# Weight loads and field 0 in ring order, field loads one by one, and more splits dealt out: a pairwise bilinear kernel on one core

## The chip, the cores and the metric

The kernel runs on one core of a Trainium2 chip. The metric is the device time of one execution in microseconds (us). Three executions before the change took 749.28, 749.29 and 749.32 us; the median is 749.29 us.

A core has a matrix engine (PE, with its weight loads as PEld), a vector engine (DVE), an activation engine (ACT), a general engine (POOL) and a sync engine (SP) that here only issues DMA transfers. Transfers run on 16 DMA engines, whoever issues them.

## What is computed

There are 1024 samples of 32 fields with 128 numbers each, and one 128 x 128 matrix for each of the 496 pairs of fields i < j. For every sample and pair, field i is multiplied by the pair's matrix, and the result is multiplied element by element with field j:

```python
v_i = inputs[:, I_IDX, :]
v_j = inputs[:, J_IDX, :]
transformed = jnp.einsum('bpd,ped->bpe', v_i, W)
return transformed * v_j
```

In float32 the inputs are 16.8 MB, the matrices 32.5 MB and the output 260 MB. Much of what follows is about the stores of that output.

## The kernel before the change

**Order of the work.** The pairs are numbered q = 0 to 495, from field i = 30 down to field 0, and for each i over j = i + 1 to 31. Field i has 31 - i pairs, and they begin at `first_q[i]`, which is (30 - i)(31 - i)/2: field 17 begins at 91, field 12 at 171, field 0 at 465. The main loop (L243) counts half-pairs u = 2q + h; each half is a tile of 128 x 512 (512 samples). `first(u)` issues the first matmuls, `second(u)` the last one and the multiplication by field j, three half-pairs later.

**Splits.** The first 15 pairs are multiplied in plain float32 (L216). All others use three faster matmuls (L219 twice, L228 once) on operands that have been split into parts: a high part, a low part and a difference. `split_w` splits a weight chunk of two pairs: one operation on ACT (L128) and three on POOL (L129 to L131). `split_x` splits one half of field i: one on ACT (L145), two on POOL (L146, L147), and the difference on DVE (L273) for fields 10 to 25 or on POOL (L151) for fields 0 to 9. All splits stand in a list `todo` with the pair from which each may be issued and its deadline; at every odd u the ready one with the earliest deadline is issued. A weight chunk is ready five pairs before its first use. A field's halves are ready one pair into the field before; for fields 1 to 11 (`SPREAD`) they are moved on by 1/5 and 3/5 of that field's length.

**Weights.** Eight pairs make one weight load of 512 KB, numbered c = 0 to 61, in a ring of three buffers (`WB`). A load of chunk c can start once the last split of the chunk that held its buffer has read it. Even chunks from 12 on (`WAPART`) are fetched in two parts (L103, L104): 448 KB issued by POOL[...], 64 KB by SP. They are asked for in the loop as soon as the last split of chunk c - 3 has been issued (L269). Odd chunks are asked for at fixed pairs `w_at`, in general at 8c - 17 (L182 to L186); chunks 55 and 57, the odd ones among the first three after `XAFTER`, come at 8c - 11. [...]

**Fields.** Fields 31 to 17 are loaded one by one at the start and through the first pairs. Fields 16 to 1 are loaded in four groups of 2 MB at pairs 52, 141, 219 and 313 (`XAT`): `load_group` fetches four fields in one transfer from a copy that the host has laid out in rows of 16 KB. Field 0 borrows one of the three weight buffers, at pair 421 (`x_at`).

**Output buffers.** A store takes four pairs, 2 MB, and is issued on ACT's queue (L263). Three output buffers (`s0` to `s2`) are always there. The four group tiles serve as output buffers too until 20 pairs before their fields are loaded (`until`), so the number falls from seven to three, for the last time at pair 293.

**Queues.** SP issues its transfers in program order, and waits at each for its buffer: the fields, the odd chunks and the 64 KB parts stand in one line. POOL issues its parts between its splits. PE, ACT, DVE and POOL also work strictly in program order.

Of the kernel before, what the change touches and what calls it, by code (L numbers as in the profile page):

```python
# [7 lines left out]
F32 = mybir.dt.float32  # L8
# [3 lines left out]
P = 128  # L12
NF = 32
NQ = NF * (NF - 1) // 2
BT = 1024
HB = 512
WC = 2
WL = 8
# [3 lines left out]
SHARED = 16  # L22
XDLAG = 10
LAG = 3
SPREAD = 12
WB = 3
WLEAD = 12
XAFTER = 54
XLEAD = 5

XG = 4
NE = 14
ROWS = 8 * NE
WAPART = tuple(range(12, 62, 2))
BACK = 3
XAT = (313, 219, 141, 52)
OWAIT = 20
SLAG = 2


# [6 lines left out]
def kernel(  # L47
# [22 lines left out]
    nc = tc.nc  # L70
# [3 lines left out]
    xpool = ctx.enter_context(tc.tile_pool(name="x", bufs=1))  # L74
# [6 lines left out]
    x_sb = {}  # L81

    def load_x(f, pieces=1, eng=None):
        if f == 0:

            t = rpool.tile([P, WL, P], F32, tag="w", name="x_0").rearrange("p q e -> p (q e)")
        else:
            t = xpool.tile([P, BT], F32, tag=f"x{f}", name=f"x_{f}")
        s = BT // pieces
        for k in range(pieces):  # L90
            (eng or nc.sync).dma_start(out=t[:, k * s : (k + 1) * s], in_=xt[f, :, k * s : (k + 1) * s])
        x_sb[f] = t

    w_raw = {}
# [3 lines left out]
    def move_on(k):  # L98

        nc.gpsimd.dma_start(out=mark[: 2 * k], in_=xt[0, : 2 * k, :16].rearrange("(b a) n -> a b n", a=k))  # L100

    def load_apart(dst, src):
        nc.gpsimd.dma_start(out=dst[:ROWS], in_=src[:ROWS].rearrange("(b a) m n -> a b m n", a=NE))  # L103
        nc.sync.dma_start(out=dst[ROWS:], in_=src[ROWS:])  # L104

    def load_group(k):
        t = xpool.tile([P, XG, BT], F32, tag=f"g{k}", name=f"x_g{k}")
        f = XG * k + 1
        nc.sync.dma_start(out=t, in_=xt[f : f + XG].rearrange("m d b -> (m d b)").rearrange("(d m b) -> d m b", m=XG, b=BT))
        for m in range(XG):  # L110
            x_sb[f + m] = t[:, m, :]

    def load_w(c, splits=(0, WL), eng=nc.sync):
        w_raw[c] = rpool.tile([P, WL, P], F32, tag="w", name=f"w_{c}")
        if c in WAPART:
            load_apart(w_raw[c], wt[c])
            return
        for a, b in zip(splits, splits[1:]):
            eng.dma_start(out=w_raw[c][:, a:b, :], in_=wt[c, :, a:b, :])

    w_s, spent = {}, []
# [17 lines left out]
    def split_x(f, a, u):  # L139

        if a == 0:
            x_s[f] = [spool.tile([P, BT], F32R, tag=t, name=f"{t}_{f}") for t in ("xh", "xl", "xd")]
        s = slice(a, a + HB)
        h, l, d = [t[:, s] for t in x_s[f]]
        nc.scalar.mul(h, x_sb[f][:, s], 1.0 - 2.0**-13)  # L145
        nc.gpsimd.tensor_tensor(l, x_sb[f][:, s], h.bitcast(F32), ALU.subtract)  # L146
        nc.gpsimd.tensor_scalar(l, l.bitcast(F32), 1.0 / EPS, 1.0, ALU.mult, ALU.mult)  # L147
        if f > NF - 2 - NATIVE - SHARED:
            later.append((min(u + XDLAG, 2 * first_q[f] + LAG - 1), d, h.bitcast(F32), l.bitcast(F32)))
        else:  # L150
            nc.gpsimd.tensor_tensor(d, h.bitcast(F32), l.bitcast(F32), ALU.subtract)  # L151
# [3 lines left out]
    first_q = {i: q for q, (i, j) in reversed(list(enumerate(pairs)))}  # L155
# [6 lines left out]
    for i in range(NF - 2 - NATIVE, -1, -1):  # L162
        for a in range(0, BT, HB):
            at = first_q[i + 1] + 1 if i < NF - 3 - NATIVE else 2
            if 0 < i < SPREAD:
                at += (NF - 2 - i) * (1 + 2 * (a > 0)) // 5
            todo.append((at, first_q[i], lambda u, i=i, a=a: split_x(i, a, u)))
    todo.sort(key=lambda t: t[1])

# [5 lines left out]
    load_w(1, eng=nc.sync)  # L175
    for f in range(NF - 5, NF - 4 - XLEAD, -1):
        load_x(f)
# [3 lines left out]
    w_at = {}  # L181
    for c in range(WB, -(-NQ // WL)):  # L182
        free = (c - WB + 1) * WL if (c - WB) * WL < nq0 else 0
        early = 0 if XAFTER < c <= XAFTER + WB else WLEAD - 6
        if c not in WAPART:
            w_at[max(c * WL - 3 * WC - 5 - early, free)] = c  # L186
    x_at = XAFTER * WL - 11
    assert x_at not in w_at and len(w_at) == NQ // WL - WB - len(WAPART)

    back = []  # L190
    w_next = list(WAPART)

    ngroup = NF // XG // 2
    group_at = {q: k for k, q in enumerate(XAT)}
    assert all(q < first_q[XG * k + XG + 1] for q, k in group_at.items())
    until = {f"g{k}": q - OWAIT for q, k in group_at.items()}
    used = {t: n - 9 for n, t in enumerate(("s0", "s1", "s2", *sorted(until, reverse=True)))}

    def out_tile(g):
# [9 lines left out]
    def first(u):  # L209
        q, h = divmod(u, 2)  # L210
        i, c = pairs[q][0], q // WC
        r = slice(q % WC * P, (q % WC + 1) * P)
        s = slice(h * HB, (h + 1) * HB)
        po[u] = ppool.tile([P, HB], F32, tag="po", name=f"po_{u}")
        if q < nq0:
            nc.tensor.matmul(po[u], w_raw[q // WL][:, q % WL, :], x_sb[i][:, s], start=True, stop=True)  # L216
        else:
            for t in (0, 1):
                nc.tensor.matmul(po[u], w_s[c][t][:, r], x_s[i][t][:, s], start=t == 0, stop=t == 1)  # L219
            nc.scalar.mul(po[u], po[u], 1.0 + EPS)  # L220

    def second(u):
        q, h = divmod(u, 2)
        i, j = pairs[q]
        r = slice(q % WC * P, (q % WC + 1) * P)
        s = slice(h * HB, (h + 1) * HB)
        if q >= nq0:
            nc.tensor.matmul(  # L228
                po[u], w_s[q // WC][2][:, r], x_s[i][2][:, s], start=False, stop=True, skip_group_check=True
            )  # L230
        g, k = divmod(q, OG)
        if k == 0 and h == 0:
            ots[g] = out_tile(g)
        nc.vector.tensor_tensor(ots[g][:, k, s], po.pop(u), x_sb[j][:, s], ALU.mult)  # L234
        if q >= NQ - 2:
            stores.append((u + SLAG, out[g, :, k, s], ots[g][:, k, s]))
        elif g == 0 or q >= NQ - OG:
            if h == 1:
                stores.append((u + SLAG, out[g, :, k], ots[g][:, k]))
        elif k == OG - 1 and h == 1:  # L240
            stores.append((u + SLAG, out[g], ots[g]))

    for u in range(2 * NQ + LAG + SLAG):  # L243
        q = u // 2
        if u < 2 * NQ:
            i, j = pairs[q]
            if u % 2 == 0 and j == i + 1 and XG * ngroup < i - 2 - XLEAD:
                load_x(i - 2 - XLEAD)
            first(u)
            if u == 2 * nq0:  # L250
                move_on(5)
            if u % 2 == 0 and q in group_at:
                load_group(group_at[q])
            if u % 2 == 1 and q in w_at:
                load_w(w_at[q])
            if u % 2 == 0 and q in back:
                move_on(16 - NE if w_next else 13)
            if u == 2 * x_at + 1:
                load_x(0)
        if LAG <= u < 2 * NQ + LAG:  # L260
            second(u - LAG)
        while stores and stores[0][0] <= u - LAG:
            nc.scalar.dma_start(*stores.pop(0)[1:])  # L263
        if u % 2 == 1:
            ready = [t for t in todo if t[0] <= q]
            if ready:
                ready[0][2](u)
                todo.remove(ready[0])
        if w_next and (XAFTER if w_next[0] == XAFTER + 2 else w_next[0] - WB) in spent:  # L269
            load_w(w_next.pop(0))  # L270
            back.append(q + BACK)
        while later and later[0][0] <= u:
            nc.vector.tensor_tensor(*later.pop(0)[1:], ALU.subtract)  # L273
    assert not todo and not later and not stores
# [32 lines left out]
```

## Time and profile before

| What | Value |
|---|---|
| Median of three executions | 749.29 us |
| Profiled execution | 752.84 us |
| Its span, first to last instruction | 751.1 us |
| PE busy | 703.7 us (94%) |
| DVE busy | 662.8 us (88%) |
| ACT busy | 625.7 us (83%) |
| POOL busy | 614.9 us (82%) |
| Moved by DMA | 310.06 MB, mean 413 GB/s |
| Mean granted PE clock | 0.981 |

The page divides the span into 40 slices of 18.8 us. Of each engine it gives the busy share, of PE also the granted clock, and of the DMA engines the busy share and what they moved. A share close to one on several engines at once says little here; what matters is which wait ends last in a given stretch. The costliest groups of instructions, with count and mean length:

| Line | Engine | What | Count | Mean ns |
|---|---|---|---|---|
| L219, L228 | PE | matmuls of the split pairs | 2886 | 393 to 396, overlapping |
| L220 | ACT | scaling between the matmuls | 962 | 583 |
| L234 | DVE | product with field j | 992 | 684 to 685 |
| L129, L130, L131 | POOL | split of a weight chunk | 241 each | 762, 416, 744 |
| L146, L147 | POOL | split of a field's half | 52 each | 1315, 675 |
| L151 | POOL | difference, fields 0 to 9 | 20 | 1288 |
| L273 | DVE | difference, fields 10 to 25 | 32 | 970 |

Of the transfers, a 2 MB store takes 12.4 us from issue to landing (median), a 512 KB weight load of SP's 10.6 us, POOL's part of an even chunk 11.8 us, and a 2 MB group of fields 18.0 us.

### The profile page before, as it was taken

The numbers are of one execution on the slowest core, as the hardware profiler recorded it, in microseconds if no ns is written. First come the engines' busy times: TensorE is split into PE (matmuls) and PEld (weight loads), VectorE is DVE, ScalarE is ACT, GpSimd is POOL, SyncE is SP. The second block draws the span as 40 slices with busy tenths as digits, with TensorE's granted clock in tenths as the row PEclk, the third lists the DMA queues.
The fourth block names the chain that finished last, engine by engine and source line by source line (L and its number), as shares of the span: only waits on it lengthen the run. The fifth ranks groups of instructions, "written<-read, shape, count | busy, mean of one in ns | idle before, by whom it ended". The sixth has DMA issues, their size and how long they took to land.

```text
span 751.1 us, 11065 instructions
## 1 busy us (share of the span) xinstructions
PE 703.7 (94%) x2946; PEld 556.8 (74%) x2946; DVE 662.8 (88%) x1024; ACT 625.7 (83%) x1256; POOL 614.9 (82%) x902
## 2 busy tenths in 40 slices
PE   7998999899999999996999979799999999889994
PEld 3576777777787788885887858688877777668883
DVE  3899999999999999986998869699888888779995
ACT  1198989889999999995999959689988889779993
POOL 1789999999999989986999968869898888797660
PEclk9999999999999999999999989899999999999997
DMA  9999999999999999999999999999999999989998
GB/s 344 430 421 430 407 428 428 426 402 414 403 420 426 426 424 423 427 419 421 427 423 427 423 416 385 426 406 414 419 426 419 408 422 405 403 340 420 419 424 344
DMA packets 32941, 310.06 MB, mean 413 GB/s; under 512 B 5104, under 2 KB 5232, under 8 KB 16752
## 3 DMA queue, kind: packets, MB, share of 16 engines
q10 hardware_dynamic: 19584, 261.10, 82.8%
q1 hardware_dynamic: 8864, 36.77, 12.3%
q0 software_dynamic: 4432, 11.48, 4.3%
q8 instruction: 24, 0.39, 0.2%
q14 instruction: 37, 0.30, 0.1%
HBM read 49.29 MB, written 260.05 MB: 412 GB/s over the span
## 4 chain that ended last, share of the span: by engine, by line
PE 65%; DMA 18%; DVE 7%; POOL 6%; issue 1%; ACT 1%; DVEq 0%; ACTq 0%; POOLq 0%
PE po L219 41%; PE po L228 20%; DMA out_dram<-ot 18%; DVE ot L234 6%; PE po L216 4%; POOL wl L129 2%; POOL xl L146 1%; POOL wd L131 1%; ACT po L220 1%; POOL xl L147 1%; DMA x<-in_xt_dram 1%; POOL xd L151 1%; POOL wd L130 0%; DVE xd L273 0%; ACT wh L128 0%
## 5 line engine op out<-in xcount | busy, mean ns | idle before, releaser
L220 ACT ACTIVATE po<-po 128x512 f32<-128x512 f32 x962 | 544.9, 583 | 90.1 <-PE po L219 51.4
L234 DVE TENSOR_TENSOR ot<-po,x 128x512 f32<-128x512 f32 x720 | 463.1, 684 | 61.6 <-DMA out_dram<-ot 33.8
L219 PE MATMUL po<-xh,wh 128*128 128x512 f32 x962 | 380.5, 396 | 19.9 <-DVE ot L234 19.8
L219 PE MATMUL po<-xl,wl 128*128 128x512 f32 x962 | 379.6, 395 | 10.9 <-POOL wl L129 9.5
L228 PE MATMUL po<-xd,wd 128*128 128x512 f32 x962 | 377.6, 393 | 1.8 <-DVE xd L273 0.9
L219 PEld LDWEIGHTS po<-xh,wh 128*128 128x128 f32 x962 | 182.5, 190 | 66.4 <-DVE ot L234 28.1
L129 POOL TENSOR_TENSOR wl<-w,wh 128x256 fp32r<-128x256 f32 x241 | 183.6, 762 | 55.8 <-ACT wh L128 51.5
L219 PEld LDWEIGHTS po<-xl,wl 128*128 128x128 f32 x962 | 182.5, 190 | 53.6 <-POOL wl L129 14.5
L228 PEld LDWEIGHTS po<-xd,wd 128*128 128x128 f32 x962 | 182.6, 190 | 41.9 <-ACT po L220 2.7
L131 POOL TENSOR_TENSOR wd<-wl,wd 128x256 fp32r<-128x256 f32 x241 | 179.4, 744 | 20.1
L234 DVE TENSOR_TENSOR ot<-po,x_g 128x512 f32<-128x512 f32 x272 | 174.6, 685 | 17.3 <-DMA out_dram<-ot 10.1
L130 POOL TENSOR_SCALAR wd<-wh 128x256 fp32r<-128x256 f32 x241 | 100.2, 416 | 20.5
L128 ACT ACTIVATE wh<-w 128x256 fp32r<-128x256 f32 x241 | 99.1, 412 | 9.9 <-DVE ot L234 5.4
L146 POOL TENSOR_TENSOR xl<-x_g,xh 128x512 fp32r<-128x512 f32 x32 | 42.1, 1315 | 0.5
L146 POOL TENSOR_TENSOR xl<-x,xh 128x512 fp32r<-128x512 f32 x20 | 26.3, 1316 | 15.8 <-ACT xh L145 15.6
L147 POOL TENSOR_SCALAR xl<-xl 128x512 fp32r<-128x512 f32 x52 | 35.1, 675 | 4.7
L216 PE MATMUL po<-x,w 128*128 128x512 f32 x60 | 30.4, 666 | 4.2 <-DMA x<-in_xt_dram 4.0
L273 DVE TENSOR_TENSOR xd<-xh,xl 128x512 fp32r<-128x512 f32 x32 | 31.0, 970 | 0.2 <-POOL xl L147 0.2
L216 PEld LDWEIGHTS po<-x,w 128*128 128x128 f32 x60 | 12.4, 212 | 21.4 <-issue 14.1
L151 POOL TENSOR_TENSOR xd<-xh,xl 128x512 fp32r<-128x512 f32 x20 | 25.8, 1288 | 1.7
L145 ACT ACTIVATE xh<-x 128x512 fp32r<-128x512 f32 x20 | 12.4, 627 | 11.5 <-DMA x<-in_xt_dram 11.4
L145 ACT ACTIVATE xh<-x_g 128x512 fp32r<-128x512 f32 x32 | 20.0, 626 | 0.0
(7 smaller groups left out, 33.8 us busy)
## 6 DMA issues: line engine op xcount, KB each, us to landing
out_dram<-ot ACTq DMA_DIRECT2D x122, 2048.0 KB, 12.4
w<-in_wt_dram SPq DMA_DIRECT2D x36, 512.0 KB, 10.6
w<-in_wt_dram POOLq DMA_DIRECT2D x25, 448.0 KB, 11.8
x_g<-in_xt_dram SPq DMA_DIRECT2D x4, 2048.0 KB, 18.0
x<-in_xt_dram SPq DMA_DIRECT2D x14, 512.0 KB, 9.4
out_dram<-ot ACTq DMA_DIRECT2D x6, 512.0 KB, 8.3
w<-in_wt_dram SPq DMA_DIRECT2D x26, 64.0 KB, 6.1
x<-in_xt_dram ACTq DMA_DIRECT2D x4, 256.0 KB, 6.0
```

The costliest lines, as they stand in the source:

```text
L128: nc.scalar.mul(h, raw, 1.0 - 2.0**-13)
L129: nc.gpsimd.tensor_tensor(l, raw, h.bitcast(F32), ALU.subtract)
L130: nc.gpsimd.tensor_scalar(d, h.bitcast(F32), EPS, 1.0, ALU.mult, ALU.mult)
L131: nc.gpsimd.tensor_tensor(d, l.bitcast(F32), d.bitcast(F32), ALU.subtract)
L146: nc.gpsimd.tensor_tensor(l, x_sb[f][:, s], h.bitcast(F32), ALU.subtract)
L147: nc.gpsimd.tensor_scalar(l, l.bitcast(F32), 1.0 / EPS, 1.0, ALU.mult, ALU.mult)
L151: nc.gpsimd.tensor_tensor(d, h.bitcast(F32), l.bitcast(F32), ALU.subtract)
L216: nc.tensor.matmul(po[u], w_raw[q // WL][:, q % WL, :], x_sb[i][:, s], start=True, stop=True)
L219: nc.tensor.matmul(po[u], w_s[c][t][:, r], x_s[i][t][:, s], start=t == 0, stop=t == 1)
L220: nc.scalar.mul(po[u], po[u], 1.0 + EPS)
L228: nc.tensor.matmul(po[u], w_s[q // WC][2][:, r], x_s[i][2][:, s], start=False, stop=True, skip_group_check=True)
L234: nc.vector.tensor_tensor(ots[g][:, k, s], po.pop(u), x_sb[j][:, s], ALU.mult)
```

## The change

There are three edits.

1. All weight chunks from 12 on, odd ones too, and field 0 are asked for in one list `ring`, in order: each when the last split that reads the buffer it takes over has been issued. Field 0 stands between chunks 54 and 55, and its own second split frees its buffer for chunk 57. Before, 57 came at pair 445, after 58.
2. Fields 16 to 1 are loaded one by one, 512 KB each, six pairs apart (`XSTEP`), highest field first, into the same four group tiles; the host no longer lays groups out in long rows. The pairs of `XAT` are those of the first load of each four.
3. The halves of fields 17 to 12 are dealt out as well (`SPREAD` 18), and the shares of the field's length are 1/5 and 1/2 in place of 1/5 and 3/5, for fields 1 to 11 too.

```diff
-SPREAD = 12
+SPREAD = 18
+WRING = 12
+XSTEP = 6
...
-    def load_group(k):
-        t = xpool.tile([P, XG, BT], F32, tag=f"g{k}", name=f"x_g{k}")
-        f = XG * k + 1
-        nc.sync.dma_start(out=t, in_=xt[f : f + XG].rearrange("m d b -> (m d b)").rearrange("(d m b) -> d m b", m=XG, b=BT))
-        for m in range(XG):
-            x_sb[f + m] = t[:, m, :]
+    group = {}
+
+    def load_group(k, m):
+        if m == XG - 1:
+            group[k] = xpool.tile([P, XG, BT], F32, tag=f"g{k}", name=f"x_g{k}")
+        f = XG * k + 1 + m
+        x_sb[f] = group[k][:, m, :]
+        nc.sync.dma_start(out=x_sb[f], in_=xt[f])
...
+        if f == 0 and a > 0:
+            spent.append("x")
...
-                at += (NF - 2 - i) * (1 + 2 * (a > 0)) // 5
+                at += (NF - 2 - i) * (2 + 3 * (a > 0)) // 10
...
-        early = 0 if XAFTER < c <= XAFTER + WB else WLEAD - 6
-        if c not in WAPART:
-            w_at[max(c * WL - 3 * WC - 5 - early, free)] = c
-    x_at = XAFTER * WL - 11
+        if c < WRING:
+            w_at[max(c * WL - 3 * WC + 1 - WLEAD, free)] = c
...
-    w_next = list(WAPART)
+    last = NQ // WL
+    ring = [*range(WRING - WB, XAFTER + 1), "x", *range(XAFTER + 1, last)]
...
-    group_at = {q: k for k, q in enumerate(XAT)}
+    group_at = {q + XSTEP * (XG - 1 - m): (k, m) for k, q in enumerate(XAT) for m in range(XG)}
...
-            if u == 2 * x_at + 1:
-                load_x(0)
...
-        if w_next and (XAFTER if w_next[0] == XAFTER + 2 else w_next[0] - WB) in spent:
-            load_w(w_next.pop(0))
-            back.append(q + BACK)
+        if ring[WB:] and ring[0] in spent:
+            ring.pop(0)
+            c = ring[WB - 1]
+            if c == "x":
+                load_x(0)
+            else:
+                load_w(c)
+            if c in WAPART:
+                back.append(q + BACK)
...
-    for f in range(1, XG * 4, XG):
-        xt[f : f + XG] = xt[f : f + XG].transpose(1, 0, 2).copy().reshape(XG, P, BT)
```

More of the change, by code (lines that the diff above doesn't have):

```diff
@@ L183 @@
         free = (c - WB + 1) * WL if (c - WB) * WL < nq0 else 0
-        early = 0 if XAFTER < c <= XAFTER + WB else WLEAD - 6
-        if c not in WAPART:
-            w_at[max(c * WL - 3 * WC - 5 - early, free)] = c
-    x_at = XAFTER * WL - 11
-    assert x_at not in w_at and len(w_at) == NQ // WL - WB - len(WAPART)
+        if c < WRING:
+            w_at[max(c * WL - 3 * WC + 1 - WLEAD, free)] = c
     back = []
-    w_next = list(WAPART)
+    last = NQ // WL
+    ring = [*range(WRING - WB, XAFTER + 1), "x", *range(XAFTER + 1, last)]
     ngroup = NF // XG // 2
-    group_at = {q: k for k, q in enumerate(XAT)}
-    assert all(q < first_q[XG * k + XG + 1] for q, k in group_at.items())
-    until = {f"g{k}": q - OWAIT for q, k in group_at.items()}
+    group_at = {q + XSTEP * (XG - 1 - m): (k, m) for k, q in enumerate(XAT) for m in range(XG)}
+    assert all(q + 5 < first_q[XG * k + m + 2] for q, (k, m) in group_at.items())
+    until = {f"g{k}": q - OWAIT for k, q in enumerate(XAT)}
     used = {t: n - 9 for n, t in enumerate(("s0", "s1", "s2", *sorted(until, reverse=True)))}
@@ L252 @@
             if u % 2 == 0 and q in group_at:
-                load_group(group_at[q])
+                load_group(*group_at[q])
             if u % 2 == 1 and q in w_at:
@@ L256 @@
             if u % 2 == 0 and q in back:
-                move_on(16 - NE if w_next else 13)
-            if u == 2 * x_at + 1:
-                load_x(0)
+                move_on(16 - NE if max(w_raw) < WAPART[-1] else 13)
         if LAG <= u < 2 * NQ + LAG:
```

## The prediction

> **What bounds the kernel now.** I read the page's slices first, then the busy times over stretches, the waits in each stretch, and last the timelines of POOL, DVE and SP where a stretch loses time.
>
> ```profile
> DMA  9999999999999999999999999999999999989998
> GB/s 344 430 421 430 407 428 428 426 402 414 403 420 426 426 424 423 427 419 421 427 423 427 423 416 385 426 406 414 419 426 419 408 422 405 403 340 420 419 424 344
> q10 hardware_dynamic: 19584, 261.10, 82.8%
> q1 hardware_dynamic: 8864, 36.77, 12.3%
> ```
>
> The DMA engines are never free, and the best slices reach 430 GB/s. 310.06 MB at 430 GB/s are 721 us, so about 30 us of the 751.1 us span are slices below that rate. Those slices fall in three stretches with three causes.
>
> Stretch A, 44 to 262 us. The waits there, and POOL's timeline:
>
> ```profile
> ACT po L220 <- PE po L219: 11.7, 14, 2.1
> PEld po L219 <- POOL wl L129: 11.5, 10, 2.5
> PE po L219 <- POOL wl L129: 7.3, 9, 2.0
> DVE ot L234 <- PE po L228: 2.7, 4, 1.4
> POOL wl L129 <- ACT wh L128: 0.7, 1, 0.7
> ```
>
> ```profile
> 195.15 0.62 POOL L103 DMA_DIRECT2D w<-in_wt_dram  x1
> 195.80 1.30 POOL L146 TENSOR_TENSOR xl<-x_g,xh 128x512 fp32r<-128x512 f32 x1
> 197.19 0.62 POOL L147 TENSOR_SCALAR xl<-xl 128x512 fp32r<-128x512 f32 x1
> 197.88 0.74 POOL L129 TENSOR_TENSOR wl<-w,wh 128x256 fp32r<-128x256 f32 x1
> ```
>
> PE waits for POOL, POOL waits once (0.7 us), and DVE never waits for a store here. POOL is the bound, back to back; DVE's full digits are its 0.685 us operations keeping PE's pace of 0.68 us a unit (the listed matmul starts of one kind lie 0.68 apart). DMA takes what comes: 406 GB/s from 150.0 to 206.5 us.
>
> Stretch B, 300 to 638 us, is the stores':
>
> ```profile
> 337.00:356.00 19.00, 13.06 (x50) 10.00 (x49) 10.96 (x18) 10.29 (x22) 11.66 (x17) 0.91 1.01 423
> 432.00:450.00 18.00, 12.91 (x48) 9.97 (x47) 10.55 (x18) 10.09 (x22) 12.56 (x19) 0.81 1.00 422
> 450.00:469.00 19.00, 19.00 (x86) 15.73 (x85) 18.87 (x29) 17.91 (x37) 15.45 (x23) 1.00 0.98 382
> 469.00:488.00 19.00, 14.84 (x58) 11.85 (x57) 12.07 (x20) 12.43 (x26) 15.46 (x24) 0.88 1.01 424
> 488.00:545.00 57.00, 57.00 (x248) 47.00 (x248) 52.11 (x81) 52.77 (x107) 47.14 (x70) 0.98 1.01 414
> ```
>
> ```profile
> 444.33 4.40 DVE L234 TENSOR_TENSOR ot<-po,x 128x512 f32<-128x512 f32 x7 [5.95 <-DMA out_dram<-ot]
> 483.35 4.40 DVE L234 TENSOR_TENSOR ot<-po,x 128x512 f32<-128x512 f32 x7 [6.09 <-DMA out_dram<-ot]
> ```
>
> (Columns: busy us and count of PE, PEld, DVE, ACT, POOL, then granted clock, DMA share, GB/s.) PE loses 5 us in each stall, yet DMA moves 422 to 424 GB/s through it: the stall itself is free. What costs is the stretch after it, at 382 and 414 GB/s, where PE restarts slowly and the stores run out. The stalls near 340 and 483 us follow the 2 MB group loads issued at 329.43 and 462.87; the one at 444 comes as output buffers fall from four to three (pair 293).
>
> Stretch C, 638 to 676 us (372 GB/s), is W chunk 55 landing late (ACT waits 2.7 us), with field 0's splits in POOL's way behind it.
>
> **What the Trainium skill says.** "DMA: Bandwidth & Descriptors", Queues, rings and completion order: an SDMA engine takes its queue rows in turn, packet by packet. The trace agrees: where 4 KB weight rows meet stores of 16 KB rows (439 to 444 us) the sum stays at 417 GB/s. The same page, "Issuing engines are not separate DMA queues", says that all issuers share 16 engines, so moving loads about adds no bandwidth; 430 GB/s in slices of very different mix agrees. "TensorE: Matmul & The Clock Gate", Part 1: after an idle window of about 3.4 us the clock halves until PE has been busy as long. Here the granted clock was 0.81 in 432 to 450 us.
>
> **The change part by part.**
>
> (1) Odd weight chunks from 13 on are asked for up to six pairs earlier in program order. But SP runs ahead and waits for the buffer: its waits at L119 for POOL wl are 365.4 us in 32. For instance chunk 55 was issued at 641.25, as the `wl` of 640.48 + 0.74 ended. The buffer's last reader is the same after the change, and the SP order of the chunks too, save at the end. Price 0 on SP; POOL's loads of even chunks keep their place. What was hidden stays hidden.
>
> (2) Field 0 in the ring: chunk 57 takes field 0's buffer (free at 664.24, as `xl` ended) instead of chunk 55's (669.01), and 58 takes the other. Chunk 57's first split is chunk of pairs 228, near 680 us, so neither was late. Price 0. If PE were ahead by 8 us it would matter; it is not.
>
> (3) Spreading fields 17 to 12. POOL's work is the same, so in a stretch that POOL fills the gain is in order alone. Today weight DMA, first half, one weight chunk, mark and second half come together: from 195.15 to the end of the next chunk at 205.0 POOL finishes two weight chunks in 9.9 us, where PE uses one in 2.72 us. It loses 9.9 - 5.4 = 4.5 us of lead and wins 2.72 - 2.02 = 0.7 us back per chunk (chunks start 2.02 us apart in a gapless run). With the new formula the second half comes two to four chunks later than now, so 1.4 to 2.8 us of lead are won back between the halves, the dip is that much shallower, and PE can run that much nearer to POOL. I take 1.5, the size of the one DVE bubble there (1.40 at 144.00). Deadline: field 17's second half began at 139.87 and was first used about 8.7 us later; four pairs of 1.36 us later still leave 3 us, against 2.0 us of `xl` work (1.31 + 0.68). After it the DMA is next in line; from 150 to 206.5 us it has room (406 against 430), so the gain passes. Range 0 to -2.8.
>
> (4) Halves of fields 11 to 1 come 2 or 3 pairs earlier. Field 1's second half (637.14 to 640.5) stands just ahead of the split that frees chunk 55's buffer. One chunk sooner, that release comes some 0.8 us earlier, out of ACT's 2.7 us wait: -0.5, range +0.3 to -1.
>
> (5) Four 2 MB loads of 16 KB rows become sixteen of 512 KB with 4 KB rows, six pairs apart. SP issues 4 x 0.33 = 1.3 us for each old 1.15: nothing. Each lands in about 10 us (the weight loads' 10.6) and is needed 12 pairs (16 us) or more later: no wait. On the DMA: q10 needs 0.828 x 751.1 / 261.10 = 2.38 us per MB, q1 with its mix 2.51; taking the 8.4 MB of groups out at q10's price leaves 2.55 for q1's small rows, so 8.4 MB get dearer by at most 8.4 x 0.17 = 1.4 us, at least 0 where they interleave. I take +0.4. In return the stores keep most of each engine's turns, the 6.09 us stall at 483 us splits into pieces of about 1.2 us (512 KB at 425 GB/s), PE stays at full clock, and the shortfall after it shrinks: 57 us x (1 - 414/425) = 1.5 us, of which I take half, -0.8. The stall at 340 us goes too, but brings nothing, as stores were queued. The one at 444 us is not touched. Range of this part -1.5 to +4.8, the upper end from the rival below.
>
> Sum: 0 + 0 - 1.5 - 0.5 + 0.4 - 0.8 = -2.4 us. The profiled execution took 752.84 us (span 751.1); the plain runs' median is 749.29. I take the difference over unchanged: 746.9.
>
> **Rivals.**
>
> *The stores swallow it.* From 206 us on DMA is at 422 to 428 GB/s, so A's gain may only lengthen the queue, and the buffers fill sooner. For: the waits for stores from 304 us on. Against: the hole at 150 to 206 us. Result: +0.4 - 0.8 remain, at about 748.9.
>
> *Single reads run into an empty store queue (slower).* A weight read that comes when few stores are queued runs all engines at once and slowly: 621 to 624 us had 302 GB/s, 457 to 460 had 320, so 0.8 us is lost against 425. The eight single loads of fields 8 to 1 would each cost that, 6.4 us, less the two bursts' own aftermath (about 2), so +4.4; with A's -1.5, C's -0.5 and the dearer rows' +0.4 that is +2.8, or 752.1. It decides from the fifth of the eight that falls into such a gap (0.8 x 5 - 2 - 1.6 = +0.4). For: three output buffers from pair 293 on. Against: while a queue exists, reads interleave at 417.
>
> *The stalls matter more than I think.* DVE's waits from the groups are 3.37 + 4.66 and 0.56 + 6.09 = 14.7 us. If half came off the end: 742. Against: DMA moved 423 GB/s through them.
>
> **How the numbers follow.** Main case 0.51, around 746.9 (745.3 to 748.5): faster 0.44, same 0.07. Swallowed 0.18: same. Slower rival 0.20: 0.18 slower, 0.02 same. Large gain 0.11: faster. Together faster 0.55, same 0.27, slower 0.18, where 0.2% (1.5 us) is what a measurement of this kernel tells from none. The range 743.4 to 751.6 leaves out the lower half of the large gain and the upper half of the slower rival, with what lies past all cases.
>
> **What would show it.** Part 3: POOL still without gaps to about 260 us, but PE's waits for `wl` in 112 to 262 us well below now, and pairs there done 1 to 2 us earlier. Part 5: no DVE wait of 6 us near 483 us, several near 1 us, clock at 1.0, and over 414 GB/s in 488 to 545 us. Parts 1 and 2: SP's issues of odd chunks still at the ends of `wl`. Wrong if PE's waits for POOL move but do not shrink, or if slices after 450 us fall below today's rates wherever an x read lies.

## The result, and the profile after

The first comparison gave 745.91 us for the changed kernel and 749.20 us for the kernel before (medians of 12 executions each), a ratio of 0.9966 with a 95% interval of 0.9946 to 0.9987. A ratio takes in all executions, so it is not the quotient of the two medians: 0.9966 stands for 2.5 us, while the medians lie 3.3 us apart. The forecast was 746.9 us against 749.29, a ratio of 0.9968. Two further comparisons on the same footing gave less: 0.9987 (0.9968 to 1.0006) and 0.9995 (0.9970 to 1.0020). Weighted by their intervals the three come to about 0.9982, give or take 0.0012, or 1.4 us faster. That is below the 1.5 us at which the forecast drew its line, and the sum of the single parts is no better known. So all three point the way that was forecast, but only the first interval leaves out no change, and the size is little more than half of the first figure. As the experiments show, the gain of the forecast's main term did not reach the end.

The page of the changed kernel, with the lines that answer to those of before:

```profile
DMA  9999999999999999999999999999999999999998
GB/s 344 426 422 430 428 428 425 428 427 420 426 422 426 422 422 429 424 425 423 425 427 424 422 427 348 417 424 425 423 427 390 424 419 421 427 422 417 424 418 330
q10 hardware_dynamic: 19584, 261.10, 83.3%
q1 hardware_dynamic: 10592, 36.77, 12.3%
```

The low slices between 75 and 206 us are gone (402 to 414 before, 420 to 428 now), and so is the one at 657 to 676 us. But slice 25, from 446 to 465 us, has fallen to 348. The span is 743.7 us against 751.1.

This 7.4 us difference of two single traces must not be read as the effect. 2.3 us of it lie before pair 20, where the two kernels do the same. The rest lies after pair 313, at about 470 us: up to there, counted from pair 20, the two are level (429.8 and 429.6 us). Counted in the same way to the end, the three traces of the changed kernel alone take 704.6, 706.2 and 709.7 us, so they differ by as much among themselves.

What waited in the changed kernel from 44 to 262 us (engine and line waited for: us in total, times, longest):

```profile
ACT po L224 <- PE po L223: 9.2, 14, 1.5
PEld po L223 <- POOL wl L133: 7.7, 11, 1.6
PE po L223 <- POOL wl L133: 3.3, 6, 1.2
PEld po L223 <- POOL xl L151: 3.0, 4, 1.7
```

PE's own waits for weight splits are down from 7.3 to 3.3 us, and POOL has no wait in the list at all: it works without a gap, as before, only in another order.

Two stretches of the changed kernel (busy us and counts of PE, PEld, DVE, ACT, POOL, then clock, DMA share, GB/s), and DVE's timeline at two places:

```profile
432.00:469.00 37.00, 31.62 (x130) 25.58 (x129) 29.71 (x46) 26.99 (x55) 26.64 (x39) 0.91 0.95 380
469.00:545.00 76.00, 72.42 (x312) 57.72 (x311) 62.37 (x103) 66.67 (x134) 64.53 (x97) 1.00 1.01 426
```

```profile
296.23 4.87 DVE L238 TENSOR_TENSOR ot<-po,x 128x512 f32<-128x512 f32 x8 [3.55 <-DMA out_dram<-ot]
...
441.94 4.40 DVE L238 TENSOR_TENSOR ot<-po,x 128x512 f32<-128x512 f32 x7 [6.26 <-DMA out_dram<-ot]
```

DVE's first long wait for a store now comes at 296 us and takes 3.55 us. In the first trace of before DVE had waited 0.94 us once by 304 us. PE arrived earlier, and met the stores' queue earlier. The stall at 444 us is still there, 6.26 us long.

### The profile page after: what moved, and what is told of

It is laid out like the page before. It is cut to its first block, busy times and chain, and to the rows that moved or that the text cites. A ratio compares the mean times of both kernels' runs of the same rounds, so it can differ in the third digit from the quotient of the medians.

```text
span 743.7 us, 11084 instructions
## 1 busy us (share of the span) xinstructions
PE 701.1 (94%) x2946; PEld 552.0 (74%) x2946; DVE 652.0 (88%) x1024; ACT 626.1 (84%) x1256; POOL 613.2 (82%) x902
## 3 DMA queue, kind: packets, MB, share of 16 engines
q1 hardware_dynamic: 10592, 36.77, 12.3%
## 4 chain that ended last, share of the span: by engine, by line
PE 49%; DMA 29%; POOL 9%; DVE 8%; issue 2%; ACT 1%; DVEq 0%; SPq 0%; POOLq 0%; ACTq 0%
PE po L223 31%; DMA out_dram<-ot 25%; PE po L232 15%; DVE ot L238 7%; DMA x<-in_xt_dram 3%; PE po L220 3%; POOL wl L133 2%; POOL wd L135 2%; POOL xl L150 2%; POOL xl L151 1%; POOL wd L134 1%; ACT po L224 1%; DVE xd L281 1%; POOL xd L157 1%; ACT wh L132 0%
## 5 line engine op out<-in xcount | busy, mean ns | idle before, releaser
L238 DVE TENSOR_TENSOR ot<-po,x 128x512 f32<-128x512 f32 x720 | 457.9, 683 | 62.0 <-DMA out_dram<-ot 33.1
L238 DVE TENSOR_TENSOR ot<-po,x_g 128x512 f32<-128x512 f32 x272 | 170.0, 682 | 20.2 <-DMA out_dram<-ot 11.3
L220 PE MATMUL po<-x,w 128*128 128x512 f32 x60 | 28.1, 625 | 4.2 <-DMA x<-in_xt_dram 4.1
## 6 DMA issues: line engine op xcount, KB each, us to landing
x_g<-in_xt_dram SPq DMA_DIRECT2D x16, 512.0 KB, 17.4
```

## The experiments

All ratios are to the kernel before, measured beside it on the same chip. "All parts" is the changed kernel. Spread only, single loads only, ring order only and all but ring order come from one chip; all parts the second time, before against itself, all but spread and all but single loads from another. Ratios from different chips are compared here only roughly.

| Kernel | Median us | Ratio | 95% interval |
|---|---|---|---|
| All parts, first | 745.91 | 0.9966 | 0.9946 to 0.9987 |
| All parts, second | 748.28 | 0.9987 | 0.9968 to 1.0006 |
| All parts, third | 747.04 | 0.9995 | 0.9970 to 1.0020 |
| Before against itself | 748.13 | 0.9993 | 0.9968 to 1.0018 |
| Spread only | 748.33 | 1.0009 | 0.9993 to 1.0026 |
| Single loads only | 747.60 | 0.9993 | 0.9974 to 1.0011 |
| Ring order only | 749.54 | 1.0010 | 0.9996 to 1.0023 |
| All but ring order | 748.80 | 1.0016 | 0.9997 to 1.0035 |
| All but spread | 748.49 | 0.9986 | 0.9970 to 1.0003 |
| All but single loads | 749.14 | 0.9995 | 0.9973 to 1.0017 |
| All parts, six groups in halves | 750.32 | 1.0005 | 0.9980 to 1.0031 |
| Lightened, before | 726.41 | 0.9682 | 0.9654 to 0.9710 |
| Lightened, spread only | 723.41 | 0.9653 | 0.9621 to 0.9685 |

To follow PE through the trace, count ACT's scaling operations (two for each pair from pair 15 on) and note when the first one of a pair starts. Times below are since pair 20, so that the start falls out:

| Kernel | to pair 168 | to pair 192 | to pair 219 | to pair 288 |
|---|---|---|---|---|
| Before, first trace | 216.0 | 248.6 | 285.3 | 388.2 |
| Before, second trace | 215.8 | 248.4 | 285.3 | 388.3 |
| Spread only | 213.9 | 246.5 | 285.0 | 388.3 |
| All parts, three traces | 213.4, 214.4, 214.1 | 246.0, 246.4, 246.1 | 286.7, 288.7, 290.0 | 387.2, 388.5, 389.6 |
| Lightened, before | 216.1 | 248.7 | 285.3 | 381.7 |
| Lightened, spread only | 213.7 | 246.3 | 282.9 | 379.4 |

### The spread alone

```diff
-SPREAD = 12
+SPREAD = 18
-                at += (NF - 2 - i) * (1 + 2 * (a > 0)) // 5
+                at += (NF - 2 - i) * (2 + 3 * (a > 0)) // 10
```

> The kernel before with only the new dealing out of the splits (fields 17 to 12 too, second halves at 1/2 of the field's length). Theory (the prediction): the dip of the weight splits' lead gets shallower, PE is 1.5 us or more ahead at pair 171, and that reaches the end: -1.5 to -2 us (ratio 0.997 to 0.998). Rival (the stores swallow it): PE is ahead by 2 to 2.6 us at pair 171, but level with before again by pair 300, as DVE waits that much longer for stores; the time changes by less than 0.7 us.

The rival's case came out, in each of its numbers: PE is 2.1 us ahead at pairs 168 and 192, level again at pair 288 (388.3 against 388.2), and the time does not change (1.0009). In fact the lead is gone by pair 219. The place where it goes, first before, then with the spread:

```profile
297.79 5.21 DVE L234 TENSOR_TENSOR ot<-po,x 128x512 f32<-128x512 f32 x8 [0.23 <-PE po L219]
```

```profile
295.50 4.87 DVE L234 TENSOR_TENSOR ot<-po,x 128x512 f32<-128x512 f32 x8 [2.34 <-DMA out_dram<-ot]
...
336.20 4.87 DVE L234 TENSOR_TENSOR ot<-po,x 128x512 f32<-128x512 f32 x8 [2.39 <-DMA out_dram<-ot]
...
345.86 3.68 DVE L234 TENSOR_TENSOR ot<-po,x 128x512 f32<-128x512 f32 x6 [4.78 <-DMA out_dram<-ot]
...
441.38 4.40 DVE L234 TENSOR_TENSOR ot<-po,x 128x512 f32<-128x512 f32 x7 [6.38 <-DMA out_dram<-ot]
```

These are the products of pairs 196 to 199, the first group for which the output buffers have fallen from five to four. Counted from pair 20 (41.34 us before, 39.07 us here), they begin 256.4 us later in both. Before, DVE waited 0.23 us for PE there; with the spread it is early and waits 2.34 us for a store. The later stalls of before, at 340, 349 and 444 us, stand here too and, counted in the same way, end 0.7 to 1.3 us earlier. So the stores decide when DVE gets its buffers. With all parts PE is even 1.4 to 4.7 us behind before at pair 219, and about level at pair 288.

### The single loads alone, the ring order alone

The edits are the diff's parts on `load_group`, `group_at` and the host's layout, and those on `w_at`, `ring` and `x_at`.

> The kernel before with only the field loads one by one, six pairs apart, rows of 4 KB. Theory: the wait of 6 us near 483 us breaks into pieces, PE keeps its clock, -0.4 us in all (ratio 0.999 to 1.000). Rival A (the stalls matter more): -2 us or better (ratio under 0.9975). Rival B (single reads meet an empty store queue): +2 us or worse, with under 400 GB/s wherever an x read lies after 330 us.

0.9993 (0.9974 to 1.0011): the theory's figure, with rival B out and rival A only just (0.9975 was its bound). From 460 to 510 us, where the last four fields are loaded, and from 326 to 352:

```profile
326.00:352.00 26.00, 25.02 (x108) 19.58 (x107) 21.71 (x37) 22.69 (x47) 24.06 (x38) 1.00 1.01 423
460.00:510.00 50.00, 46.78 (x202) 37.09 (x201) 40.47 (x65) 43.52 (x88) 43.91 (x65) 1.00 1.01 424
```

No rate under 400 beside the single reads, and PE at full clock. DVE's waits for stores in 450 to 545 us are nine with the longest 2.1 us, where before had three with the longest 6.1. Their sum is larger, not smaller: 10.2 against 7.0 us.

> The kernel before with only the weight chunks and field 0 asked for in ring order. Theory: SP's waits end with the same splits, chunk 57 merely comes about 5 us sooner, nothing waits for it: 0 (ratio 0.999 to 1.001). Rival: the reads of chunks 57 and 58 no longer fall together in the stretch where stores run out, and the hole at 669 to 674 us shrinks: -1 to -2.5 us.

1.0010 (0.9996 to 1.0023): nothing, as forecast. The rival's gain is excluded.

### Each part left out

> The changed kernel with the old order of weight loads and of field 0 (both other parts stay). Theory: as the changed kernel, ratio to before 0.9955 to 0.998. Rival (ring order matters): 1 us or more slower than the changed kernel, ratio 0.998 or above, with a low stretch in the DMA rate where chunks 57 and 58 are read.

1.0016 (0.9997 to 1.0035) misses the theory's range and lies in the rival's, but no low stretch where chunks 57 and 58 are read goes with it: from 655 to 680 us this kernel moved 407 GB/s, against 411 and 418 in two traces of all parts. All parts were not measured on this chip, and the spread alone and the ring order alone gave about 1.001 there as well. Whether the ring order helps beside the other two parts is left open.

> The changed kernel with the old dealing out of the splits (ring order and single field loads stay). If the spread's gain is swallowed by the stores before pair 300: the same as the changed kernel within 0.15%. If the spread pays: 1.5 us or more slower than the changed kernel.

0.9986 (0.9970 to 1.0003) beside 0.9987 for all parts on the same chip: the spread pays nothing that shows here either.

> The changed kernel with fields 16 to 1 in groups of 2 MB (ring order and spread stay). If the single loads are worth 0.4 us net, as predicted: within 0.15% of the changed kernel. If they only pay together with the ring order, which keeps them in step with the weight loads: 1.5 us or more slower than the changed kernel.

0.9995 (0.9973 to 1.0017), 0.08% over all parts: within the bound of the first case, though intervals of 0.2% either way do not shut out the second.

> The changed kernel once more, beside the ones that leave one part out. If its first result holds on this chip: 0.995 to 0.998. If the three single results (each within 0.2% of none) simply add up: 0.999 to 1.002.

0.9987 lies between the two expectations, nearer to the second.

### The kernel before against itself

> The kernel before against itself, for the measurement's own spread and for a second trace: ratio 0.998 to 1.002. If the stretches after 444 us (rates, place of the stalls, chunk 55's late landing) differ from the first trace by 2 us or more, then differences of that size between single traces there say nothing about the change.

The ratio is 0.9993 (0.9968 to 1.0018), on the chip where all parts gave 0.9987: there the change is not told from nothing. The second trace of before, in the stretches where the first was compared with the changed kernel:

```profile
432.00:469.00 37.00, 31.87 (x131) 25.85 (x130) 29.09 (x45) 27.94 (x57) 27.75 (x42) 0.91 0.98 396
469.00:545.00 76.00, 70.55 (x301) 57.88 (x300) 63.47 (x98) 64.24 (x130) 61.74 (x92) 0.96 0.99 411
638.00:676.00 38.00, 35.76 (x155) 28.94 (x155) 34.84 (x56) 30.71 (x61) 32.73 (x49) 1.00 0.99 399
```

From 638 to 676 us it moved 399 GB/s; the first trace had 372. Over 38 us that is 2.6 us, from one execution of the same program to another. The 419 GB/s of that stretch after the change are thus not shown to be an effect of it; the two other traces of all parts have 414 and 403. The rates of 396 and 411 GB/s in the two others, however, agree with the first trace (402 and 416).

### With fewer stores

To test what swallows the spread's gain, 15 of the 124 output groups are not stored (every eighth, 31.5 MB, so that part of the output is missing), in before and in before with the spread:

```diff
         elif k == OG - 1 and h == 1:
-            stores.append((u + SLAG, out[g], ots[g]))
+            if g % 8 != 7:
+                stores.append((u + SLAG, out[g], ots[g]))
```

> The kernel before without the store of every eighth output group (15 groups, 31.5 MB, 10% of the traffic, are left out), so that the DMA engines have room. If the stores bound the stretch after 300 us: DVE's waits for stores nearly gone, PE full from 262 us on, about 712 to 718 us. If PE or POOL bound it: within 5 us of before.

> The same lightened kernel with the new dealing out of the splits. If the spread's gain of 2 us was swallowed by the stores: now it stays, PE 2 to 2.6 us ahead of the lightened kernel at pair 288 and at the end, and the time 1.5 to 2.5 us under it. If it was lost to something else (PE, POOL, the later second halves): no more than 0.7 us.

The lightened kernels took 726.41 and 723.41 us: 3.0 us apart in the medians, a little more than the 1.5 to 2.5 us expected (0.9682 and 0.9653, whose intervals overlap). The traces are clearer: the one with the spread is 2.4 us ahead at pairs 168 and 192, and still 2.3 us ahead at pair 288, where with all stores it was level. DVE's waits for stores fell from 43.9 us in the first trace of before to 8.0 and 8.4 us. From 262 to 432 us neither has any DVE wait for a store; the lightened kernel with the spread waited for these:

```profile
PEld po L219 <- POOL wl L129: 3.7, 4, 1.5
DVE ot L234 <- PE po L228: 3.1, 4, 1.3
ACT po L220 <- PE po L219: 2.2, 3, 1.1
PE po L219 <- POOL wl L129: 2.0, 3, 1.1
POOL wl L129 <- ACT wh L128: 0.7, 2, 0.5
```

So it is the stores that take the gain. The level of 712 to 718 us that was expected was missed by 8 us or more. PE was to be full from 262 us on, but in the lightened kernel before it was busy 406.6 of the 414 us from 262 to 676; where the rest of the difference lies stays open.

### An attempt at the hole after 442 us

The deepest slice of the changed kernel follows the step from four output buffers to three. The six groups around it were stored in halves:

```diff
+        elif g in HALVES:
+            if k % 2 == 1 and h == 1:
+                stores.append((u + SLAG, out[g, :, k - 1 : k + 1], ots[g][:, k - 1 : k + 1]))
```

> The changed kernel with output groups 73 to 78 (pairs 292 to 315, around the step from four output buffers to three) stored in two halves of 1 MB each, so that a store can start before the whole buffer is filled. If the hole in the stores after the stall at 442 us (374 and 386 GB/s in 432 to 469 us) is lost time: the rate there back above 410 GB/s and 2 to 4 us under the changed kernel, ratio to before 0.993 to 0.996. If it is made up later anyway: as the changed kernel.

It failed: 394 GB/s in 432 to 469 us instead of the 410 expected, and 1.0005 (0.9980 to 1.0031). It beats neither kernel.

### The size once more

> The changed kernel a third time, for the size alone: the first two ratios are 0.9966 (0.9946 to 0.9987) and 0.9987 (0.9968 to 1.0006). If the gain is the 0.3% of the first: under 0.998. If it is what the parts alone gave, about nothing: 0.999 to 1.001. In between: 0.998 to 0.999.

0.9995 (0.9970 to 1.0020): nearer to nothing than to the first result.

## Why the prediction was right or wrong

**Parts 1 and 2, ring order (0): right for the ring order alone (1.0010), open beside the other parts (1.0016 without it).** The trace of the changed kernel shows it for the one load that moved. POOL and, below it, SP:

```profile
654.79 1.30 POOL L150 TENSOR_TENSOR xl<-x,xh 128x512 fp32r<-128x512 f32 x1
...
660.11 0.73 POOL L133 TENSOR_TENSOR wl<-w,wh 128x256 fp32r<-128x256 f32 x1
```

```profile
656.11 0.33 SPq L123 DMA_DIRECT2D w<-in_wt_dram  x1
660.87 0.33 SPq L106 DMA_DIRECT2D w<-in_wt_dram  x1
```

Chunk 57 is issued at 656.11, as field 0's second `xl` ends (654.79 + 1.30), and the 64 KB of chunk 58 at 660.87, as chunk 55's last `wl` ends (660.11 + 0.73). Both waits end where the buffers' readers end; the program order of the requests decided nothing here. Nobody waited for chunk 57 before either.

**Part 3, the spread (-1.5): the mechanism right, the step after it wrong.** The order of POOL's work (the splits, its weight transfers and the small transfer `mark`, L100, that it issues after each of these) gained what was forecast and more: 2.1 us alone, 1.4 to 2.6 us with all parts, with POOL as full as before. From 112 to 262 us PE's waits for `wl` fell from 5.4 to 1.5 us. The deadline was missed narrowly: field 17's second half began at 141.51 us, 2.06 us ahead of the matmul that reads it instead of 3 us, and PE waited for it:

```profile
143.57 0.50 PE L223 MATMUL po<-xl,wl 128*128 128x512 f32 x1 [0.27 <-POOL xl L151]
```

The forecast took its 8.7 us to the start of ACT's scaling; in the same trace the matmul that reads the half came 8.3 us after the split began. What failed is "After it the DMA is next in line; from 150 to 206.5 us it has room (406 against 430), so the gain passes." The room was used, 424 GB/s in that stretch. But the stores of the later pairs need the engines as well, and at 422 to 428 GB/s there is little to be made up after 206 us. With the spread alone the 2.1 us are still there at pair 199 and 0.2 us are left at pair 210: they have become a wait for an output buffer. It was the first rival, *the stores swallow it*, that described this part; it was given 0.18. The lightened kernels settle it: with 10% less traffic that wait is absent and the 2.3 us stay.

**Part 4, earlier second halves (-0.5): not shown.** ACT's wait for chunk 55 was 2.7 and 5.1 us in the two traces of before, and 0, 0.3 and 0 in three of all parts. But it was 0.5 us with all but the spread as well, 2.5 us with all but the ring order, and 1.2 to 1.8 us with any one part alone. It does get shorter, for a reason that the runs do not single out.

**Part 5, single loads (+0.4 - 0.8): the sum agrees as far as 0.2% tells (0.9993 alone), the gain after the stall not shown.** The stall near 483 us broke up as forecast: between 470 and 515 us the longest wait for a store is 4.1 to 7.4 us in the five traces with 2 MB groups, and 2.3 to 2.6 us in the three of all parts. The clock stayed at 1.00. The dearer rows did not show: q1 took 12.3% of either span. From 469 to 545 us the three traces of all parts ran at 424 to 426 GB/s, against 411 and 416 before. But the spread alone and the ring order alone, both with 2 MB groups, ran at 424 there as well, so the single loads are not shown to be the cause. And from 432 to 469 us, the stretch around the stall at 444 us that was "not touched", all parts ran at 372 to 380 GB/s, against 396 and 402 before. Over both stretches together that is 407 to 411 GB/s against 406 and 411: nothing in sum. First before, then the spread alone, then the third trace of all parts:

```profile
432.00:469.00 37.00, 31.91 (x132) 25.70 (x131) 29.42 (x46) 28.00 (x58) 28.01 (x42) 0.91 0.99 402
469.00:545.00 76.00, 71.84 (x305) 58.85 (x304) 64.18 (x101) 65.20 (x132) 62.60 (x94) 0.96 1.01 416
```

```profile
432.00:469.00 37.00, 32.54 (x131) 26.41 (x131) 29.09 (x44) 28.01 (x57) 27.97 (x43) 0.91 0.96 389
469.00:545.00 76.00, 71.94 (x313) 57.93 (x312) 62.62 (x103) 66.67 (x134) 65.32 (x99) 1.00 1.01 424
```

```profile
432.00:469.00 37.00, 31.16 (x128) 24.98 (x127) 28.70 (x45) 27.49 (x55) 27.01 (x41) 0.91 0.92 372
469.00:545.00 76.00, 71.96 (x310) 57.23 (x309) 62.18 (x101) 65.90 (x134) 63.75 (x95) 1.00 1.01 424
```

Two small terms were mis-sized without harm. A single load kept SP for 1.15 us (median), not 0.33, and landed after 17.4 us, not ten. Nothing waited for either.

The slower rival, single reads in an empty store queue, fell: with the single loads alone the rates beside them are 423 and 424 GB/s. The deep slice from 446 to 465 us does not speak for it, since the hole there is over by 458 us, and the first single read of that group is issued at 460.85 us.

**The sum.** -2.4 us was forecast; by its ratio the first comparison gave -2.5, all three together -1.4. That the first agreed so well is partly chance, since the largest term of the sum is shown not to reach the end. Where the remaining 1.4 us come from, if they are there at all, stays open: each part alone is within 0.1% of nothing with intervals of about 0.2% either way, and the intervals of the three kernels with two parts also take in no change.

## What to carry to other kernels

When one engine fills an early stretch and the stores fill the rest, a gain in the early stretch may do no more than lengthen the queue, as here: ask not whether the next resource has room in the same stretch, but whether it is ever idle after it. The quick test is to take an eighth of the stores away and see whether the gain comes back. Before two single traces are compared, take a second trace of the same kernel, and mark the stretches in which it differs by itself.

## What the runs showed of the hardware

- A single field load of 512 KB in 4 KB rows took a median of 17.4 us from issue to landing, though weight loads of the same size and rows took 11.0 us in the same trace. So the length of the rows alone is not the reason. Each of the sixteen was issued within 1.3 us of another load of SP's, and landed 5.9 to 8.3 us after that one; the two other traces of all parts show the same. In three places two field loads that stand six pairs apart in the program (about 8 us) went out together, since both stood in SP's line behind a weight load:

```profile
100.51 0.33 SPq L123 DMA_DIRECT2D w<-in_wt_dram  x1
100.89 1.95 SPq L115 DMA_DIRECT2D x_g<-in_xt_dram  x2
```

- The 417 GB/s from 439 to 444 us, with loads and stores under way together, show that their sum holds. In what order an engine takes their packets, no run here shows.
- Two executions of one program differ by 2.5 us before pair 20 (41.3 us in the first trace of before, 38.9 us in its second), in a stretch in which nothing of the change takes part, and executions of either kernel took some 744 to 755 us. Repeats of one comparison moved its ratio by 0.3%.
